# Three moves in the order of work: an early norm, an output's differences, and pinned stretch differences in a two-layer attention kernel

## The chip, the cores and the metric

The kernel runs on one core of a Trainium2 chip. The metric is the device time of one execution in microseconds (us). A core has five instruction queues that matter here: TensorE (PE, matmuls, with its weight loads listed as PEld), VectorE (DVE), ScalarE (ACT), GpSimd (POOL) and SyncE (SP, which issues most DMAs). Each works through its own queue in order and waits on semaphores of the others.

## The reference

The input x is (8, 512, 32, 32) in float32: 8 images of 512 channels and 1024 positions. Two layers follow each other, both with a residual.

```python
# layer 0, 8 heads of 64 channels, group norm over 32 groups
h = group_norm(x); qkv = w_qkv @ h + b_qkv
weight = softmax(q^T k / sqrt(64));  a = weight @ v
x = x + w_proj @ a + b_proj
# layer 1, one head of 512 channels, group norm over 8 groups
h = group_norm(x); q, k, v = w_q h, w_k h, w_v h
x = x + w_p @ (softmax(q^T k / sqrt(512)) v) + b_p
```

## The kernel before

**Products.** Most matrix products (queries, keys, values, projection, layer 1's scores and values) are made with seven block products instead of eight, which needs sums and differences of the blocks first. `image_factors` (it calls `right_sums`, L165) makes the eight differences of an activation of four channel tiles: steps 0 and 1 give t1, 2 and 3 give t2, 4 and 5 overwrite a quarter of the image itself, 6 and 7 give t4. Each step is one VectorE subtraction of 128x512. `inner_factors` (L411) makes differences of these again on GpSimd, for keys and queries. `wino` runs the seven products in a given order, evicts PSUM as it goes, takes a list of `hooks` (one for each product, run after its matmuls are issued) and leaves its last two products, 4 and 3, to be issued after the first product of the next stage (`tail`). Layer 1 uses two products of weights, m (query and key weights) and z (projection and value weights), made once.

**Stages.** `prologue` prepares the weights and makes image 0's v, q, k. Its end, which the change touches, is: the second image's norm (`norm1`, whose statistics are done by then), the transposes of layer 1's value weights (`natural`, L70, into four PSUM banks `tr_wv`), their copies into SBUF (`natv`, L718, two by VectorE and two by ScalarE), the product z (`ps_wz`, 32 matmul passes), the rest of the norm, and the bias products. `group_mean` is a small matmul over the statistics (`gmean`), a copy (L115) and three operations on 128x4 elements (L117, L119, L121). `affine` is another small matmul (`gvar`), one VectorE operation (L126) and four GpSimd operations (L128 to L134).

Then a loop over the images b makes layer 0's attention of image b, with work of other stages between its steps. `attention0` has 8 steps (4 head pairs, two halves of the positions). One step is 16 score matmuls (`sc`), 8 exponentials on ScalarE (`e`, L594), 7 running sums on VectorE (`sum`, L596 and L598), 16 matmuls with the values (`av`), and then the column sums on PE (`sums`), which read the last running sum and whose reciprocal (`rc`, L559) goes out and back by DMA as a row to scale the output on GpSimd (L617). PE issues each matmul in several passes. `extra` is a list of 16 lists of work, one behind the scores and one behind the values of each step. For image 0 it holds the preparation of two weights, the normalization of image 1 (ScalarE, L140), and the eight stretch differences of image 1 (`t_h`, `h`). For a later image it holds layer 1's input of the image before, its stretch differences, and the first four differences of the output a (`t_a`, `a`, L960).

After attention, image 0 makes image 1's values (`values`, stage `psb_v` and others), then the projection (`psa_p`, `psb_p`, `psc_p`) whose block products read the eight differences of a, then image 1's keys and queries. A later image makes its projection and layer 1 of the image before.

**What sets the order.** Matmuls are pinned to the program's order by `keep_in_program_order`. So are some operations of other engines. All others may be moved by the framework's planner, which places an instruction of an engine where it expects its operands. The differences of a are pinned to the program's order before the change, the stretch differences are not.

Of the kernel before, what the change touches and what calls it, by code (L numbers as in the profile page):

```python
# [29 lines left out]
def two_attention_blocks_kernel(  # L30
# [8 lines left out]
    nc = tc.nc  # L39
    B, C, T = x.shape  # L40
    KC = C // P
# [134 lines left out]
    def main_path(ctx):  # L176
# [11 lines left out]
        def pair_tile(name):  # L188
            return big_tile(name, (P, 2, HT))

        def acc_tile(name):
            return ps_acc.tile([P, HT], F32, tag="acc", name=name)
# [509 lines left out]
        def ps_tile(n, name):  # L702
            return acc_tile(name) if n == "acc" else ps_pools["abc".index(n)].tile([P, HT], F32, tag="ps", name=name)
# [7 lines left out]
        def natural(wt, nm, banks):  # L711
            ts_ = [pair_tile(f"nat{nm}_{h}") for h in range(2)]
            t = [ts_[o // 2][:, o % 2, :] for o in range(KC)]
            pt = [ps_tile(banks[o // 2], f"tr_w{nm}_{o}") for o in range(KC)]
            for kc in range(KC):
                for o in range(KC):
                    transpose(pt[o][:, ts(kc, P)], wt[kc][:, ts(o, P)], ident)
            spread(lambda o, copy: tc.keep_in_program_order(copy(t[o], pt[o])), KC)  # L718
            return t
# [34 lines left out]
        def prologue():  # L754
            raw_k = raw("k", 5)
            raw_q = raw("q", 4)
            h0 = [load_x(0, c, "h0") for c in range(KC)]
            first = {n: prepare(n) for n in "vqk"}
            wk = natural(raw_k, "k", ("a", "b"))
            wq = natural(raw_q, "q", ("c", "acc"))  # L760
            norm = GroupNorm(0, "0_0", pinned=True)
            for c in range(KC):
                norm.stats(c, h0[c])
            hf, steps = image_factors(h0, "h0_0")

            def normed():
                norm.affine(acc_tile("gvar_0_0")[:, :KC])
                for c in range(KC):
                    norm.apply(nc.scalar if c % 2 else nc.gpsimd, h0[c], h0[c], c)

            product(
                wq, wk, "m", {6: lambda: norm.group_mean(acc_tile("gmean_0_0")[:, :KC]), 9: normed},
            )
            raw_v = raw("v", 6)
            raw_p = raw("p", 7)
            for f in first["v"][1]:
                f()
            background.extend(steps)
            for n in "qk":
                background.extend(first[n][1])  # L780
            v = by_token(weight_factors(first["v"][0]), hf, "v0_0", middle=(2, 5, 6, 7), back=4)
            finish()
            run_background(len(background))
            keep("v", first["v"][0])
            x1 = [load_x(1, c, "x1") for c in range(KC)] if B > 1 else []
            norm1 = GroupNorm(0, "0_1")
            background.extend(lambda c=c: norm1.stats(c, x1[c]) for c in range(len(x1)))
            q = conv(weight_factors(first["q"][0]), hf, pcols("bq0"), "q0_0")
            keep2("q", first["q"][0])
            keep2("k", first["k"][0])  # L790
            t, steps = prepare("m")
            k = conv(weight_factors(first["k"][0]), hf, pcols("bk0"), "k0_0", hooks=[[], [], [], [], steps])
            finish()
            keep("m", t)
            keep2("m", t)
            norm1.group_mean(acc_tile("gmean_0_1")[:, :KC])
            raw_p0 = raw("p0", 3)
            wv = natural(raw_v, "v", "bc")
            product(wv, raw_p, "z")
            norm1.affine(acc_tile("gvar_0_1")[:, :KC])  # L800
            bias = bias_products([(wk, "bq1"), (raw_p, "bv1"), (raw_p0, "bv0")])
            later = []
            for n in "pz":
                t, steps = prepare(n)
                later.append(steps)
                later.append([lambda n=n, t=t: keep(n, t), load_weight])
            later.append([
                lambda: tc.keep_in_program_order(nc.vector.tensor_copy(ubias, bias[0])),
                lambda: tc.keep_in_program_order(nc.vector.tensor_add(obias[1], bias[1], pcols("bp1"))),
                lambda: tc.keep_in_program_order(nc.vector.tensor_add(obias[0], bias[2], pcols("bp0"))),  # L810
                load_weight,
            ])
            return v, q, k, norm1, later

        psum_pools("first", 2)
        v, q, k, norm0, later = prologue()
# [127 lines left out]
        for b in range(B):  # L944
            extra = [[] for _ in range(2 * 2 * KC)]
            for i, fs in enumerate(later):
                extra[i] += fs
            later = []
            h, loads, applies = [], [], []
            if b > 0:  # L950
                h, loads, applies = begun(load_again, norm1, b - 1, "h1")
            elif B > 1:
                h, loads, applies = begun(load_x, norm0, 1, "h0")
            for f in loads:
                f()
            for i, f in enumerate(applies):
                extra[2 * i + 1].append(f)
            a = channel_tiles(f"a0_{b}")

            af, steps = image_factors(a, f"a_{b}", lambda *t: tc.keep_in_program_order(nc.vector.tensor_sub(*t)))  # L960

            if b > 0:
                hf, t = image_factors(h, f"h1_{b - 1}")
                extra[0] += late
                for i, fs in enumerate((t[:1], t[1:2], (t[2], t[4]), (t[6], t[3]), (t[5], t[7]), steps[:2], steps[2:4])):
                    extra[2 * i + 3] += fs
            elif B > 1:
                hf, t = image_factors(h, "h0_1")
                for i, fs in enumerate((t[:2], (t[2], t[4]), (t[6], t[3]), (t[5], t[7]))):
                    extra[2 * i + 7] += fs  # L970
            psum_pools(f"attention_{b}", 1)
            scaled = attention0(b, q, k, v, a, extra)
            if b > 0:
                for f in steps[4:7]:
                    f()
            psum_pools(f"products_{b}", 2)
            xt = [load_x(b, c, "x") for c in range(KC)]
            if b > 0:

                inner, sums2 = inner_factors(hf, f"h1_{b - 1}", tc.keep_in_program_order)  # L980
                for f in sums2:
                    f()
                norm1, stats = projection(b, af, xt, [scaled, steps[7]])
                gf = layer1_scores(b - 1, hf, inner)
                if b + 1 < B:
                    h, loads, applies = begun(load_x, norm0, b + 1, "h0")
                else:
                    h, loads, applies = begun(load_again, norm1, b, "h1")
                ahead = [loads, *([f] for f in applies)]
                _, *means, affine = norm_hooks(norm1, f"1_{b}")  # L990
                hooks = [[], [], [lambda: background.extend(stats)]], [[], [], *means], affine
                layer1_rest(b - 1, hf, gf, hooks, ahead)
                if b + 1 < B:
                    hf, steps = image_factors(h, f"h0_{b + 1}")
                    background.extend(steps)
                    v, f, norm0 = values(b + 1, hf)
                    q, k, late = keys_and_queries(b + 1, f, norm0, ())
            elif B > 1:
                v, f, norm0 = values(1, hf, [[], steps[:2], steps[2:4], steps[4:6], [steps[6], scaled, steps[7]]])
                norm1, stats = projection(0, af, xt)  # L1000
                hooks = norm_hooks(norm1, "1_0")
                hooks[0].append(lambda: background.extend(stats))
                q, k, late = keys_and_queries(1, f, norm0, hooks)
            else:
                for f in (*steps[:7], scaled, steps[7]):
                    f()
                all_background()
                norm1, stats = projection(0, af, xt)
                finish()
                background.extend(stats)  # L1010
                for f in sum(norm_hooks(norm1, "1_0"), []):
                    f()
                h, loads, applies = begun(load_again, norm1, 0, "h1")
                for f in loads + applies:
                    f()
        hf, steps = image_factors(h, f"h1_{B - 1}")
# [199 lines left out]
```

## Time and profile before

| | |
|---|---|
| median of 3 runs | 2898.86 us (2898.63 to 2899.46) |
| profiled execution | 2901.33 us |
| its span | 2899.5 us |
| PE busy | 2876.1 us |
| DVE, ACT, POOL busy | 2004.1, 922.4, 703.8 us |

The page gives each engine's busy time as a share of the span. The list of waits says who waited for whom, with total, number and longest. A timeline line has the start, the length, the engine, the line, the operation and its tiles, and in brackets the idle time before it and what ended that. A line with xN is a run of N instructions of one kind.

### The profile page before, as it was taken

The page shows a single profiled execution, that of the slowest core. Times are in us where ns is not written, and L with a number is a line of the kernel's source. Part 1 is how long each engine was busy: PE and PEld are TensorE (multiplying, and loading weights), DVE is VectorE, ACT ScalarE, POOL GpSimd, SP SyncE. Part 2 cuts the span into 40 slices and gives each one's busy share as a digit, 9 for nine tenths or more (in the row PEclk, how much of TensorE's full clock was granted, in tenths as well). Part 3 has the DMA queues.
Part 4 walks back from the last instruction along what each step waited for, and adds up shares of the span by engine and source line. Part 5 has one row for each costly group of instructions (what it writes and reads, how often), then busy time and mean ns, then how long its engine had stood idle before and what let it go on. Part 6 is the DMA issues. An engine that isn't in the chain of part 4 may idle for free. (4 is left out here: it accounts for less than half of the span.)

```text
span 2899.5 us, 30282 instructions
## 1 busy us (share of the span) xinstructions
PE 2876.1 (99%) x11132; PEld 1556.2 (54%) x11132; DVE 2004.1 (69%) x2753; ACT 922.4 (32%) x1201; POOL 703.8 (24%) x781
## 2 busy tenths in 40 slices
PE   9999999999999999999999999999999999999999
PEld 5335635566355653556535574356743558345544
DVE  5487787666876678765786657876588665886555
ACT  1252353214532155220552115421163212632110
POOL 2113224032140321403214122232124131140000
PEclk9999999999999999999999999999999999999999
DMA  8622403033031230322213232122311223022201
GB/s 278 223 107 89 176 17 123 32 133 147 19 142 62 107 126 26 131 92 96 107 48 109 92 120 86 48 106 96 139 68 44 105 103 143 27 75 75 95 0 67
DMA packets 91586, 280.91 MB, mean 97 GB/s; under 512 B 10595, under 2 KB 36387, under 8 KB 82470
## 3 DMA queue, kind: packets, MB, share of 16 engines
q1 hardware_dynamic: 89638, 276.61, 26.1%
q10 hardware_dynamic: 1792, 2.29, 0.2%
q8 instruction: 90, 1.47, 0.2%
q14 instruction: 66, 0.54, 0.1%
HBM read 225.93 MB, written 52.93 MB: 96 GB/s over the span
## 5 line engine op out<-in xcount | busy, mean ns | idle before, releaser
L598 DVE TENSOR_TENSOR sum<-sum,e 128x1024 f32<-128x1024 f32 x384 | 519.0, 1351 | 37.9 <-ACT e L594 0.5
L594 ACT ACTIVATE e<-sc 128x1024 f32<-128x1024 f32 x512 | 476.8, 1053 | 74.1 <-PE sc L67 74.1
L67 PE MATMUL sc<-q,k 64*128 64x512 f32 x2048 | 458.3, 596 | 0.0
L67 PE MATMUL av<-e,v 128*64 128x512 f32 x2048 | 453.6, 595 | 0.0
L67 PEld LDWEIGHTS sc<-q,k 64*128 64x128 f32 x2048 | 193.2, 186 | 238.4 <-ACT e L594 105.4
L67 PEld LDWEIGHTS av<-e,v 128*64 128x64 f32 x2048 | 141.4, 137 | 304.3 <-issue 302.3
L561 POOL TENSOR_TENSOR all_recs<-all_recs,rc 128x256 f32<-128x256 f32 x72 | 63.6, 883 | 616.7 <-DVE rc L559 608.9
L617 POOL TENSOR_TENSOR a<-a,r 128x512 f32<-128x512 f32 x56 | 114.1, 2037 | 261.3 <-DMA r<-rows 247.1
L559 DVE RECIPROCAL rc<-sums 128x256 f32<-128x256 f32 x72 | 126.4, 1756 | 57.2 <-PE sums L67 37.7
L612 ACT COPY a<-av 128x512 f32<-128x512 f32 x64 | 37.5, 585 | 305.6 <-PE av L67 305.6
L596 DVE TENSOR_TENSOR sum<-e,e 128x1024 f32<-128x1024 f32 x64 | 78.4, 1224 | 59.0 <-ACT e L594 59.0
L67 PE MATMUL psa_sc<-g,h 128*128 128x512 f32 x256 | 115.2, 595 | 0.0
L648 ACT ACTIVATE e<-e 128x512 f32<-128x512 f32 x96 | 59.7, 629 | 168.5 <-DVE e L647 168.5
L67 PE MATMUL psa_av<-e,z 128*128 128x512 f32 x256 | 113.3, 595 | 0.0
L128 POOL TENSOR_TENSOR rstd<-ve,mhalf 128x4 f32<-128x4 f32 x16 | 36.2, 2261 | 267.8 <-DVE ve L126 267.8
L140 ACT ACTIVATE h<-h,b,s 128x1024 f32<-128x1024 f32 x62 | 78.5, 1268 | 57.7 <-DMA h<-in_x 45.2
L411 POOL TENSOR_TENSOR inner_h<-h,inner_h 128x256 f32<-128x256 f32 x112 | 95.6, 856 | 2.7
L411 POOL TENSOR_TENSOR inner_h<-h 128x256 f32<-128x256 f32 x56 | 57.0, 1019 | 151.3 <-PE psc_av L67 151.3
L444 POOL TENSOR_TENSOR k<-k,k 128x256 f32<-128x256 f32 x28 | 20.1, 728 | 303.6 <-DVE u_k L439 303.6
L67 PEld LDWEIGHTS psa_sc<-g,h 128*128 128x128 f32 x256 | 48.1, 190 | 60.2 <-issue 54.5
L67 PEld LDWEIGHTS psa_av<-e,z 128*128 128x128 f32 x256 | 48.0, 190 | 57.3 <-issue 55.7
L652 POOL COPY sum<-e 128x1024 f32<-128x1024 f32 x8 | 8.8, 1101 | 283.6 <-ACT e L648 283.6
(324 smaller groups left out, 5001.4 us busy)
## 6 DMA issues: line engine op xcount, KB each, us to landing
x<-in_x SPq DMA_DIRECT2D x36, 512.0 KB
h<-in_x SPq DMA_DIRECT2D x32, 512.0 KB
spill<-x SPq DMA_DIRECT2D x32, 512.0 KB
h<-spill SPq DMA_DIRECT2D x32, 512.0 KB
x<-spill SPq DMA_DIRECT2D x32, 512.0 KB
out<-x SPq DMA_DIRECT2D x64, 256.0 KB
w_p<-sums_p SPq DMA_DIRECT2D x8, 1792.0 KB
r<-rows SPq DMA_DIRECT2D x112, 128.0 KB
```

The lines of the kernel that those rows point to most:

```text
L67: tc.keep_in_program_order(nc.tensor.matmul(*args, **kw))
L128: nc.gpsimd.tensor_tensor(rstd, ve, mhalf, ALU.pow)
L140: tc.keep_in_program_order(nc.scalar.activation(dst, src, AF.Identity, bias=b, scale=s))
L411: pin(nc.gpsimd.tensor_tensor(dst, x, y, ALU.subtract))
L559: nc.vector.reciprocal(rc, sums)
L561: nc.gpsimd.tensor_tensor(all_recs, all_recs, rc, ALU.add)
L594: nc.scalar.activation(e, sc, AF.Exp, scale=(C // 8) ** -0.5)
L596: nc.vector.tensor_add(total, es[0], e)
L598: nc.vector.tensor_add(total, total, e)
L612: nc.scalar.copy(dst, av)
L617: nc.gpsimd.tensor_tensor(dst, dst, r, ALU.mult)
L648: nc.scalar.activation(dst, dst, AF.Exp, scale=scale)
```

## The change

Three edits move work and leave the number of instructions as it is.

```diff
@@ prologue
             keep2("m", t)
-            norm1.group_mean(acc_tile("gmean_0_1")[:, :KC])
             raw_p0 = raw("p0", 3)
             wv = natural(raw_v, "v", "bc")
+            norm1.group_mean(acc_tile("gmean_0_1")[:, :KC])
             product(wv, raw_p, "z")
@@ for b in range(B)
-            af, steps = image_factors(a, f"a_{b}", lambda *t: tc.keep_in_program_order(nc.vector.tensor_sub(*t)))
+            here = lambda *t: tc.keep_in_program_order(nc.vector.tensor_sub(*t))
+            af, steps = image_factors(a, f"a_{b}", here)
             if b > 0:
-                hf, t = image_factors(h, f"h1_{b - 1}")
+                hf, t = image_factors(h, f"h1_{b - 1}", here)
...
             elif B > 1:
-                hf, t = image_factors(h, "h0_1")
+                hf, t = image_factors(h, "h0_1", here)
...
-                v, f, norm0 = values(1, hf, [[], steps[:2], steps[2:4], steps[4:6], [steps[6], scaled, steps[7]]])
+                v, f, norm0 = values(1, hf, [[], [], [], [], [*steps[:7], scaled, steps[7]]])
```

- The mean of the second image's norm is taken after the transposes and copies of the value weights instead of before them. On PE the one small matmul moves behind 16 transposes; on VectorE its four operations move behind two copies.
- The differences of image 0's output a, which stood behind products 2, 5, 6 and 7 of image 1's values in groups of two and one, all stand behind product 7.
- The stretch differences of every image are pinned to the program's order. In the built order of VectorE the differences of a step now stand behind the step's last running sum, two at most in a step; before, the planner had put some of them ahead of the last sum (two in image 0's steps at `sum_0_1_1`, `sum_0_2_0` and `sum_0_2_1`, two in one step of each later image, the fifth of eight, and one in two others). Image 0's last two move from an earlier step to the one of `sum_0_3_1`, those of a later image from the fifth step to the sixth. The eight differences of a, after the change, stand in one row behind the first evictions of the values, with one multiplication and two evictions (`v_1_0`, `v_1_1`) among them.

The orders of ScalarE, GpSimd and SP are the same in both kernels, their line numbers aside.

## The prediction

> **What bounds the kernel now.** I read the page first, then TensorE's own list of waits, then the timelines of TensorE, VectorE and GpSimd around each wait.
>
> ```profile
> span 2899.5 us, 30282 instructions
> PE   2876.1 (99%) x11132; PEld 1556.2 (54%) x11132; DVE 2004.1 (69%) x2753; ACT 922.4 (32%) x1201; POOL 703.8 (24%) x781
> ```
>
> TensorE (PE) is busy 99% of the span, so only 23.4 us lie outside its work. No other engine can matter unless it makes PE wait, and a change that leaves the matmuls alone can win only those waits. PE's waits, longest in total first:
>
> ```profile
> PE ps_wz L67 <- issue: 4.4, 1, 4.4
> PE tr_wk L70 <- DMA rawk<-in_w: 3.7, 1, 3.7
> PE psb_v L67 <- DVE u_v L238: 3.6, 1, 3.6
> ```
>
> The second is the first load of the run. The first and third are two single stalls that the change aims at. The first, on PE's, VectorE's and GpSimd's timelines:
>
> ```profile
> 100.54 1.64 PE L70 MATMUL tr_wv<-ident,rawv 128*128 128x128 f32 x13 [0.34 <-DVE k L387]
> 106.56 3.75 PE L67 MATMUL ps_wz<-rawp,natv 128*128 128x512 f32 x4 [4.38 <-issue]
> ```
> ```profile
> 100.59 1.21 DVE L117 TENSOR_TENSOR d<-mv,gmean 128x4 f32<-128x4 f32 x1
> 101.83 2.00 DVE L119 TENSOR_TENSOR d<-d 128x4 f32<-128x4 f32 x1
> 103.86 1.99 DVE L121 TENSOR_TENSOR dv<-d,mv 128x4 f32<-128x4 f32 x1
> 105.78 1.27 DVE L718 COPY natv<-tr_wv 128x512 f32<-128x512 f32 x2
> ```
> ```profile
> 97.53 8.30 POOL L306 TENSOR_TENSOR prepare_m<-prepare_m 128x896 f32<-128x896 f32 x4 [23.89 <-DVE prepare_m L286]
> ```
>
> The transposes of the value weights end at 102.18, and their copies out of PSUM (L718) stand on VectorE behind three 4-column operations of the second image's norm. These take 1.2 to 2.0 us instead of the 0.16 us that the same lines take at 684 us: each ends where one of GpSimd's four 2.07 us operations ends. PE resumes 0.11 us after the first copy. It then runs slowly, which the clock column (after POOL, 0.50 against 1.00) shows:
>
> ```profile
> 106.50:112.30 5.80, 5.74 (x7) 2.50 (x8) 0.55 (x1) 0.00 (x0) 0.00 (x0) 0.50 0.86 257
> 112.30:122.80 10.50, 10.50 (x26) 4.59 (x25) 0.00 (x0) 1.75 (x3) 0.00 (x0) 1.00 0.66 201
> ```
>
> Second stall, VectorE and the last GpSimd operation of that stretch:
>
> ```profile
> 258.00 5.60 DVE L960 TENSOR_TENSOR t_a<-a 128x512 f32<-128x512 f32 x2
> 263.53 0.68 DVE L238 TENSOR_TENSOR u_v<-psb_v,t_v 128x512 f32<-128x512 f32 x1
> ```
> ```profile
> 261.21 1.85 POOL L411 TENSOR_TENSOR inner_h<-t_h,inner_h 128x256 f32<-128x256 f32 x2
> ```
>
> Two differences of image 0's attention output take 5.60 us, against 1.24 us for two of them at 270.47, after GpSimd has ended (263.06). The eviction u_v that PE waits for stands behind them.
>
> A third loss is not in the list of waits, as most of it is too short. PE's sums (the column sums of one attention step) follow each other by 14.65 us, but by 14.86 to 14.88 in ten steps: those whose sums start at 185.22, 200.08, 214.94 in image 0, and one in each later image (414.64, 768.06, and so on). One of them on PE, and VectorE's order there:
>
> ```profile
> 185.22 0.64 PE L67 MATMUL sums<-sum,ones 128*32 128x256 f32 x8 [0.15 <-DVE sum L598]
> ```
> ```profile
> 182.74 1.28 DVE L170 TENSOR_TENSOR t_h<-h 128x512 f32<-128x512 f32 x2
> 183.95 1.22 DVE L598 TENSOR_TENSOR sum<-sum,e 128x1024 f32<-128x1024 f32 x1
> ```
>
> Two stretch differences stand ahead of the step's last sum, which ends at 185.17. PE needed it at about 185.0.
>
> [...] L117 to L121 and L960 wait as above, while L115 (PSUM input) takes 0.15 us and a statistics pass at 247.6 takes 0.63 us with GpSimd busy. [...] The trace agrees on the halving (0.50 after a 4.38 us gap, back to 1.00 near 112.3) and shows that a 3.63 us gap at 260.6 did not trigger it[...].
>
> **The change, part by part.**
>
> *Norm behind the copies.* The mean's matmul goes behind the transposes, and its four VectorE operations behind the two copies. The transposes still wait for VectorE's k (ends 100.48), so they end at 102.18 as before. The first output is complete near 101.83, and VectorE is free: copy one runs from about 101.88 to 102.55 (0.67 us[...]), copy two to 103.15; ScalarE's two end at 103.06 as now. The moved matmul (0.28 us) lies in this wait. PE starts ps_wz at 102.55 + 0.08 = 102.63 instead of 106.56: 3.93 us. The gap left is about 0.4 us, so the clock stays at 1.00 and the 32 passes take 32 x 0.4295 = 13.74 us (0.43 us spacing from 112.5 on), where now 106.56 to 122.77 = 16.21 us: another 2.47 us. Sum 6.40 us. The norm's operations then run from 103.15, and waiting for GpSimd's ends at 103.77 and 105.84 give dv by about 106; its reader, the variance matmul, comes at 102.63 + 13.74 = 116.4. Cover 10 us. GpSimd's four norm operations (1.9 us to 125.6) and SP's queue follow PE: their orders don't change. SP is held by the stores of the prepared weights until 111.16; the first product store would be ready at 110.3, and its load of prepare_p is read 12 us later. If copy one did wait for GpSimd (until 103.77), the part gives 1.2 us less in the first term.
>
> *Differences of image 0 behind the last value product.* The eight subtractions are issued after value product 7 instead of between 5, 6 and 7. VectorE's new order puts statistics passes (single input) before u_v. The second u_v starts at 258.0 + 2 x 0.6 = 259.2 and ends at 259.9, before PE's first half of product 7 ends at 258.74 + 8 x 0.2147 = 260.46. PE goes on there instead of at 264.26: 3.80 us. Next late could be psc_p, whose bank is freed by an eviction behind the whole row. From 259.2 I count, by pitches in this stretch: to w_v 262.4, second w_v 263.1 to 263.7, two evictions to 264.9, then seven subtractions, one multiplication, two evictions and the last subtraction, 11 x 0.6 = 6.6 us, to 271.5, and the eviction needed ends at 272.15. PE asks for it at 260.46 + 1.72 + 3 x 3.45 = 272.5. So 0.35 us of slack; before, PE lost 0.14 us at its start and about 0.1 at its second pass. Sum 3.80 + 0.2 = 4.0 us. GpSimd has ended by 263.1, so the subtractions from 264.9 on take 0.68 us.
>
> *Stretch differences pinned behind the sums.* Same 64 instructions, two per step at most, behind the step's last sum. Ten steps fall from 14.86 to 14.65 us: 10 x 0.21 = 2.1 us. Nothing that PE reads then stands behind them: the reciprocal starts after PE's sums, and sum end 183.95 + two at 0.6 = 185.2 is earlier than that. The pinned subtractions of the output (L960) already stand like that, in steps of 14.65 us. Steps with one difference ahead of the last sum (the one at 723.89) keep 14.65 us, so only the ten with two are counted. Image 0's last two differences move to the step near 229, still before GpSimd first uses them at 239.6; a later image's move from the fifth step to the sixth, ahead of the same GpSimd work. Their ScalarE inputs are applied one step or more ahead.
>
> Together 6.40 + 4.0 + 2.1 = 12.5 us. The profiled execution took 2901.33 us (span 2899.5 and 1.8 around it), which gives 2888.8. The median of the runs shown is 2898.86, 2.47 us lower, which is just the half-clock loss. [...] I take it that the timed runs don't pay it: 2898.86 - 10.0 = 2888.9. If they do, and profiling cost the 2.47 us, it is 2886.4.
>
> **Rivals.**
> - The timed runs pay for the half clock: 2886.4. For it: the three runs agree within 0.8 us, so all or none had it. [...]
> - A wait takes the place of one removed: psc_p behind the row of subtractions (0.35 us of slack only), or copy one behind GpSimd. Losing 1.7 to 4.0 us of the 12.5: 2890.5 to 2892.8.
> - Slower: GpSimd's inner differences are still running when the nine two-input operations come in a row. At (5.60 - 1.24) / 2 = 2.2 us extra each that is 19.8 us, less 0.35 of slack, 19.4 against 12.5 gained: +6.9 us, 2905.8 on the median. It decides when GpSimd ends past 264.9 by most of the row; the trace has it end at 263.06, and nothing delays it.
> - The pins do little, or the order on VectorE is not what hurts, and two parts fail: 2893 to 2897, within 0.2%.
>
> **How the numbers follow.** Forecast 2888.8: 0.63, own range 2887.8 to 2889.9. Half clock paid: 0.14. Replaced wait: 0.15. Two parts fail: 0.05. Slower: 0.03. The range 2885.9 to 2891.3 takes the first two and part of the third, about 0.84. A measurement of this kernel can tell about 0.2% (5.8 us) from no change, so faster means below 2893.1: 0.63 + 0.14 + 0.15 = 0.92, same 0.05, slower 0.03.
>
> **What would show it.** After: ps_wz without a 4.4 us wait, at clock 1.00 throughout, starting near 102.6; dv ending near 106; no psb_v wait on u_v; psc_p starting 4.0 us earlier relative to the attention's last sums; all sums of an attention at 14.65 us; PE's share outside its work down from 23.4 to about 15. Wrong if psc_p or the first score of attention waits on VectorE or a DMA for over 1 us, or if the steps with pinned differences exceed 14.65 us.

## The result, and the profile after

| | before | after |
|---|---|---|
| median in one job (7 runs each) | 2899.46 us (2896.69 to 2901.82) | 2888.66 us (2887.46 to 2889.58) |
| profiled execution | 2901.33 us | 2888.66 us |
| its span | 2899.5 us | 2886.8 us |
| span outside PE's work | 23.4 us | 15.2 us |

The ratio is 0.9962 (95% interval 0.9951 to 0.9974). A later job, with 33 runs of before, gave 2888.75 against 2901.91 us, 0.9953 (0.9939 to 0.9966). The two profiled spans differ by 12.7 us.

The head of the page of after, first the span and then busy time by engine:

```profile
span 2886.8 us, 30280 instructions
...
PE 2871.6 (99%) x11132; PEld 1555.1 (54%) x11132; DVE 2001.5 (69%) x2753; ACT 922.8 (32%) x1201; POOL 704.2 (24%) x781
```

The number of working instructions of each engine is the same; the total is lower by two semaphore instructions. PE's busy time fell by 4.5 us, of which 2.8 us are passes that no longer run at half clock (a granted clock of 0.50, below). Its list of waits (total, number, longest) has lost both stalls:

```profile
PE tr_wk L70 <- DMA rawk<-in_w: 3.8, 1, 3.8
PE psa_v L67 <- issue: 0.8, 1, 0.8
PE psb_v L67 <- DVE w_v L238: 0.5, 1, 0.5
PE tr_wv L70 <- DVE k L387: 0.5, 1, 0.5
PE ps_wm L67 <- DVE natq L718: 0.5, 1, 0.5
PE ps_wz L67 <- ACT natv L718: 0.4, 1, 0.4
```

*First place.* PE's timeline of after:

```profile
100.33 1.64 PE L70 MATMUL tr_wv<-ident,rawv 128*128 128x128 f32 x13 [0.51 <-DVE k L387]
101.81 0.28 PE L67 MATMUL gmean<-mv,gm 128*128 128x4 f32 x2
102.48 13.97 PE L67 MATMUL ps_wz<-rawp,natv 128*128 128x512 f32 x32 [0.39 <-ACT natv L718]
116.29 0.28 PE L67 MATMUL gvar<-dv,gm 128*128 128x4 f32 x2
```

VectorE's timeline beside it:

```profile
101.69 1.29 DVE L718 COPY natv<-tr_wv 128x512 f32<-128x512 f32 x2 [1.41 <-PE tr_wv L70]
102.89 0.15 DVE L115 COPY gmean<-gmean 128x4 f32<-128x4 f32 x1
103.08 0.57 DVE L117 TENSOR_TENSOR d<-mv,gmean 128x4 f32<-128x4 f32 x1
103.68 2.00 DVE L119 TENSOR_TENSOR d<-d 128x4 f32<-128x4 f32 x1
105.71 0.16 DVE L121 TENSOR_TENSOR dv<-d,mv 128x4 f32<-128x4 f32 x1
```

The copies go first and take 0.69 and 0.68 us although GpSimd is in its long row then. The norm behind them still waits for GpSimd (0.57 us in L117, 2.00 us in L119), but nobody waits for it: dv is there at 105.87 and its reader `gvar` comes at 116.29. The clock column (after POOL) says 1.00 where before said 0.50:

```profile
106.50:112.30 5.80, 5.80 (x15) 2.58 (x14) 0.00 (x0) 0.86 (x2) 0.00 (x0) 1.00 0.88 264
```

From the 13 transposes to the first score of attention it is 26.41 us before (100.54 to 126.95) and 19.70 after (100.33 to 120.03): 6.71 us.

*Second place.* VectorE and then PE in after:

```profile
251.60 0.67 DVE L238 TENSOR_TENSOR u_v<-psb_v,t_v 128x512 f32<-128x512 f32 x1
...
257.18 1.28 DVE L960 TENSOR_TENSOR t_a<-a 128x512 f32<-128x512 f32 x2
...
263.79 0.67 DVE L375 TENSOR_TENSOR v<-psc_v,u_v 128x512 f32<-128x512 f32 x1
```
```profile
251.19 3.62 PE L67 MATMUL psb_v<-w_v,h 128*128 128x256 f32 x16
...
264.98 3.60 PE L67 MATMUL psc_p<-t_a,w_p 128*128 128x512 f32 x8
```

The 16 passes of product 7 run in one piece, and psc_p starts without a wait 0.52 us after the eviction that frees its bank (263.79 + 0.67 = 264.46). GpSimd's last difference ends at 255.24, so the row from 257.18 on takes 0.6 us a piece. From image 0's last sums to psc_p it is 32.31 us before and 28.28 after; to the next image's first sums 111.57 and 107.42: 4.15 us.

*Third place.* Two of the sums in after that stood 14.86 us apart before:

```profile
178.08 0.64 PE L67 MATMUL sums<-sum,ones 128*32 128x256 f32 x8
192.74 0.64 PE L67 MATMUL sums<-sum,ones 128*32 128x256 f32 x8
```

The distance is 14.66 us, and 14.65 to 14.66 in every attention. Ten steps of about 0.21 us more are gone, 2.11 us.

6.71 + 4.15 + 2.11 = 13.0 us, against 12.7 us between the spans. One late start in after is of the size of the rest: `psb_k` at 1713.11 us, 0.36 us later against the matmuls ahead of it than in before, behind VectorE's `u_k`.

### The profile page after: what moved, and what is told of

It reads as the page before. It is cut to its first block, busy times and chain, and to the rows that moved or that the text cites. A ratio compares the mean times of both kernels' runs of the same rounds, so it can differ in the third digit from the quotient of the medians.

```text
span 2886.8 us, 30280 instructions
## 1 busy us (share of the span) xinstructions
PE 2871.6 (99%) x11132; PEld 1555.1 (54%) x11132; DVE 2001.5 (69%) x2753; ACT 922.8 (32%) x1201; POOL 704.2 (24%) x781
## 4 chain that ended last, share of the span: by engine, by line
PE 98%; issue 1%; DVE 1%; DMA 0%; POOL 0%; SPq 0%; ACT 0%; DVEq 0%; POOLq 0%
PE sc L67 16%; PE av L67 16%; PE psb_sc L67 6%; PE psb_av L67 6%; PE psa_av L67 4%; PE psa_sc L67 4%; PE psc_av L67 4%; PE psc_sc L67 4%; PE psb_z L67 3%; PE psb_p L67 3%; PE psb_v L67 3%; PE psb_k L67 3%; PE psb_g L67 2%; PE psb_q L67 2%; PE psa_p L67 2%; PE psa_z L67 2%
```

## The experiments

The theory: three separate stalls, each taken away by its own edit, and a half clock that the stalls bring with them. Rivals: only the first edit works and the others ride on it; the timed runs never paid the half clock; the order on VectorE isn't what hurts but GpSimd is; the number of differences ahead of the last sum doesn't matter. Each kernel is given with its median and with that of before in its own job.

### One part alone

**The norm alone**, on before:

```diff
-            norm1.group_mean(acc_tile("gmean_0_1")[:, :KC])
             raw_p0 = raw("p0", 3)
             wv = natural(raw_v, "v", "bc")
+            norm1.group_mean(acc_tile("gmean_0_1")[:, :KC])
```

> Only the first part: the second image's mean behind the value weights' transposes and copies. Theory (the three parts are separate stalls, each worth its own sum): the 4.38 us wait ahead of ps_wz falls to about 0.4 us and PE's clock stays at 1.00 through ps_wz, so the stretch from the transposes to the first attention score is 6.7 us shorter than in the profile of before; the wait of psb_v on u_v (3.6 us) stays, and ten sums stay at 14.86 us. Timed: 4 to 6.7 us under before, depending on how many runs of before pay the half clock. Rival (what is won here is given back at the next stall, as GpSimd's inner differences come earlier against VectorE's work): the wait on u_v grows by several us and the time falls by less than 3 us.

Measured: 2896.27 us against 2901.98, ratio 0.9981 (0.9975 to 0.9988). PE's wait in the second place stays:

```profile
PE psb_v L67 <- DVE u_v L238: 3.7, 1, 3.7
```

Only the first gap went: ps_wz starts after 0.4 us at clock 1.00. But this execution runs at half clock from 258.2 us for 3.41 us, after the second gap. The profiled execution of before did not do that.

**The differences of image 0 alone**, on before:

```diff
-                v, f, norm0 = values(1, hf, [[], steps[:2], steps[2:4], steps[4:6], [steps[6], scaled, steps[7]]])
+                v, f, norm0 = values(1, hf, [[], [], [], [], [*steps[:7], scaled, steps[7]]])
```

> Only the second part: the differences of image 0's output behind the last value product. Theory: the 3.6 us wait of psb_v on u_v goes, psc_p starts 4.0 us earlier against the last sums of image 0's attention, the half clock at ps_wz stays. 4.0 us under before. Rival (the row of differences makes psc_p late instead): psc_p waits for VectorE for over 1 us and the gain is under 3 us.

Measured: 2896.56 us against 2901.98, ratio 0.9984 (0.9977 to 0.9990). Now the first wait stays and the second is gone; psc_p starts 28.28 us after the last sums, as in after.

```profile
PE ps_wz L67 <- issue: 4.4, 1, 4.4
```

**The pins alone**, on before: `here` given to `image_factors(h, ...)` for both kinds of image.

> Only the third part: stretch differences pinned behind the sums. Theory: all sums of an attention follow each other by 14.65 us instead of 14.86 in ten steps, 2.1 us under before, the two single stalls stay. Rival (the pins do nothing of their own, the ten late sums have another cause, such as the exponentials): ten steps stay at 14.86 us and the time stays within 0.5 us.

Measured: 2900.67 us against 2901.98, ratio 0.9995 (0.9987 to 1.0004). By time alone this is inconclusive. By the trace it isn't: all distances between the sums of an attention are 14.65 or 14.66 us, where before has ten of 14.86 to 14.88, and both other waits are there in full.

```profile
PE ps_wz L67 <- issue: 4.4, 1, 4.4
PE psb_v L67 <- DVE u_v L238: 3.7, 1, 3.7
```

The three medians lie 5.7, 5.4 and 1.3 us under before, 12.4 together. Within the noise they add up to the whole, and by the traces each stall goes with its own edit and stays without it: none rides on another.

**After once more**, unchanged, in a job with 33 runs of before:

> The kernel after, unchanged, beside many runs of before on one chip. The three parts measured alone were worth 5.7, 5.4 and 1.3 us, together 12.4. If the parts are independent: 12 to 13 us under the median of before, and a mean clock of 0.999 in its timed runs where before has 0.998. If they overlap: clearly less than 12.

Measured: 2888.75 us (2887.61 to 2889.48) against 2901.91, 13.2 us less.

### Why the copies were late

**GpSimd held back.** The order of before on VectorE, but GpSimd's four operations for m wait for the copies, by one added 128x1 operation that reads them:

```diff
-            keep2("m", t)
             norm1.group_mean(acc_tile("gmean_0_1")[:, :KC])
             raw_p0 = raw("p0", 3)
             wv = natural(raw_v, "v", "bc")
+            held = small.tile([P, 1], F32, tag="held", name="held")
+            tc.keep_in_program_order(nc.gpsimd.tensor_tensor(held, wv[0][:, :1], wv[2][:, :1], ALU.add))
+            keep2("m", t)
```

> Before's order on VectorE (the norm's mean ahead of the copies), with GpSimd's four sums of the m weights held back until the copies are done by one more GpSimd operation on 128x1 elements that reads two of the copies. Theory [...]: the three norm operations take about 0.16 us each, the copies start as soon as the transposes end, the wait ahead of ps_wz is about 0.4 us, the clock stays at 1.00: 4 to 6.7 us under before, the same as moving the norm. Rival (the order itself costs it, or the operations wait for their own inputs): they still take 1.2 to 2 us and the wait ahead of ps_wz stays at 4.4 us.

VectorE, with the norm still ahead of the copies:

```profile
99.92 0.16 DVE L117 TENSOR_TENSOR d<-mv,gmean 128x4 f32<-128x4 f32 x1
100.12 0.16 DVE L119 TENSOR_TENSOR d<-d 128x4 f32<-128x4 f32 x1
100.31 0.17 DVE L121 TENSOR_TENSOR dv<-d,mv 128x4 f32<-128x4 f32 x1
101.22 1.29 DVE L718 COPY natv<-tr_wv 128x512 f32<-128x512 f32 x2 [0.74 <-PE tr_wv L70]
```

0.16, 0.16 and 0.17 us instead of 1.21, 2.00 and 1.99. So GpSimd's row was the cause of these lengths and the order on VectorE only decided who paid.

The kernel took 2898.03 us against 2901.89, ratio 0.9986 (0.9980 to 0.9993): 3.9 us less, and not the 5.7 us of the norm alone. In its profile one step of attention takes 16.24 us instead of 14.88. SP's stores of GpSimd's sums are issued until 114.93 us (until 111.09 with the norm alone). The load of w_p, which waits for another store (`sums_p`), comes at 146.67 instead of 142.59, and behind it in SP's queue the loads of the rows `r` with which GpSimd scales the output. GpSimd then runs three operations back to back beside VectorE's sums of that step. GpSimd, VectorE, and PE at the end of the step:

```profile
169.25 1.26 POOL L617 TENSOR_TENSOR a<-a,r 128x512 f32<-128x512 f32 x1 [10.40 <-DVE sum L598]
170.48 1.71 POOL L561 TENSOR_TENSOR all_recs<-all_recs,rc 128x256 f32<-128x256 f32 x1
172.15 2.26 POOL L617 TENSOR_TENSOR a<-a,r 128x512 f32<-128x512 f32 x1
```
```profile
168.01 8.80 DVE L598 TENSOR_TENSOR sum<-sum,e 128x1024 f32<-128x1024 f32 x5
```
```profile
179.21 0.64 PE L67 MATMUL sums<-sum,ones 128*32 128x256 f32 x8 [1.52 <-DVE sum L598]
```

Three of these five sums take 2.25, 1.57 and 2.11 us. In before, where only one GpSimd operation falls into the same five sums, one takes 2.12 us and the others 1.23, 7.44 us in all. The 1.36 us between 8.80 and 7.44 are what the step is longer by: holding one piece of GpSimd's work back put later GpSimd work in VectorE's way. Moving the norm leaves GpSimd's work, and the stores that wait for it, where they were.

### The half clock in timed runs

**First gap filled.** 32 transposes of the identity, which feed nothing, are added behind `natural` in before:

```diff
             wv = natural(raw_v, "v", "bc")
+            warm = acc_tile("warm")
+            for i in range(32):
+                transpose(warm[:, ts(i % 4, P)], ident, ident)
```

> Before, with 32 more transposes of the identity on PE (3.6 us at 0.114 us each, read by nobody) in the gap between the value weights' transposes and ps_wz. The stall stays, ps_wz starts at about 106.6 as before. Theory (the half clock comes from the idle gap): PE's clock stays at 1.00, ps_wz takes 13.8 us and not 16.6, so the profile shows the first attention score 2.8 us earlier than before; timed, 2.8 us under before if every run of before pays the half clock, 1 to 1.5 us if about half of them do, 0 if the timed runs don't. Rival (the slow passes of ps_wz come from VectorE's late second copy or from data not landed): ps_wz stays at 16.6 us.

PE's timeline: useful work starts as late as in before (6.07 us after the 13 transposes, 6.02 in before) and then runs at full clock.

```profile
102.23 3.66 PE L70 MATMUL warm<-ident 128*128 128x128 f32 x32
106.82 13.97 PE L67 MATMUL ps_wz<-rawp,natv 128*128 128x512 f32 x32 [0.94 <-issue]
120.63 0.28 PE L67 MATMUL gvar<-dv,gm 128*128 128x4 f32 x2
```

From ps_wz to gvar it is 13.81 us. In before it is 16.64 (the same 32 distances). So the half clock cost 2.83 us in the profiled execution of before. The time was 2900.44 us against 2901.98, ratio 0.9996 (0.9988 to 1.0005): inconclusive, and in this execution the second gap brought 3.41 us of half clock of its own.

**Both gaps filled.** So the second gap was filled too, with 30 transposes between the two halves of product 7 (`v0_1`), and 36 in the first:

```diff
+                if (name, p, i) == ("v0_1", 7, 1):
+                    warm = acc_tile("warm2")
+                    for n in range(30):
+                        transpose(warm[:, ts(n % 4, P)], ident, ident)
```

> Before, with 36 extra transposes of the identity in the first gap and 30 in the second, which fill the gaps and feed nothing. Theory A (the timed runs of before pay for half clock after both gaps): the trace has clock 1.00 from 10 us to the end, both starts of useful work as late as in before, and the time is 2.5 to 4.5 us under before, although the kernel does more. Theory B (timed runs don't pay, as the prediction inferred): within 1 us of before.

Measured: 2899.00 us (2898.21 to 2900.52) against 2901.91, ratio 0.9990 (0.9983 to 0.9996). A kernel with 66 matmuls more is 2.9 us faster. The clock is at 1.00 after both gaps, and the useful work starts as late as in before:

```profile
106.09 13.97 PE L67 MATMUL ps_wz<-rawp,natv 128*128 128x512 f32 x32 [0.49 <-issue]
...
260.99 1.99 PE L67 MATMUL psb_v<-w_v,h 128*128 128x256 f32 x8 [0.39 <-DVE u_v L238]
```

So the timed runs of before do pay for half clock, 2.9 us (1.2 to 4.9 by the interval), and 2888.75 is 10.3 us under this kernel: the stalls themselves.

The traces also show how the 2.9 us divide. With the differences alone, the pins alone and both gaps shorter (next), half clock lasts 3.41 us after the first gap, and from ps_wz to gvar it is 15.31 to 15.45 us: 1.5 to 1.6 us of cost. The 2.83 us, after 6.83 us of half clock, stand in the profiled execution of before alone. That execution paid nothing at the second gap, where the norm alone, the pins alone and the first gap filled paid 1.6 us (33.9 us from the last sums to psc_p, 32.31 in before). 1.5 and 1.6 make 3.1. It fits that filling the first gap alone took 1.5 us off, and that the first two parts alone took off 5.7 and 5.4 us: 3.9 of stall and 1.5, 4.0 and 1.6.

**Both gaps shorter.** 12 transposes at the start of the first gap and 6 in the second leave 3.09 and 3.00 us. In the clock record of before, the clock changes 28, 30 and 846 steps of 3.413 us after its first full value; such a step is what the expectation calls a window:

> Before, with 12 extra transposes at the start of the first gap and 6 at the start of the second, which leave gaps of about 3.0 and 2.9 us, under 3.4. If half clock needs one whole window of 3.41 us idle: clock 1.00 throughout, and the same time as with both gaps filled. If it goes by the share of idle time in a window: half clock after at least one gap, and a time nearer to that of before.

Measured: 2903.28 us against 2901.91, ratio 1.0003 (0.9995 to 1.0011): no gain. Stretches of the trace (start and end, length, busy time of PE, PEld, DVE, ACT and POOL, granted clock, DMA share, GB/s):

```profile
107.70:111.20 3.50, 3.48 (x5) 1.69 (x6) 0.52 (x1) 0.00 (x0) 0.00 (x0) 0.56 0.82 244
...
264.10:267.60 3.50, 3.49 (x9) 2.78 (x10) 3.50 (x7) 0.00 (x0) 0.00 (x0) 0.54 0.00 0
```

Half clock follows both gaps (0.56 and 0.54 in these stretches), though PE was idle for only 3.09 and 3.00 us. So a whole step of 3.413 us of idle time was not needed.

### How many differences, and where

**One pair early.** After, with two of the eight differences of a back behind product 2:

```diff
-                v, f, norm0 = values(1, hf, [[], [], [], [], [*steps[:7], scaled, steps[7]]])
+                v, f, norm0 = values(1, hf, [[], steps[:2], [], [], [*steps[2:7], scaled, steps[7]]])
```

> After, with only the first two of the eight differences of image 0's output put back behind value product 2. Theory (what hurt was that the first pair meets GpSimd's row of inner differences ahead of u_v): the wait of psb_v on u_v comes back in full, 3.5 to 4 us, and the time is 4 us over after. Rival (the loss grows with the number of differences issued early): a quarter of it, about 1 us.

Measured: 2894.37 us against 2901.89, ratio 0.9974 (0.9965 to 0.9984), 5.7 us over the first median of after (2888.66). VectorE:

```profile
250.46 5.60 DVE L960 TENSOR_TENSOR t_a<-a 128x512 f32<-128x512 f32 x2
255.99 0.68 DVE L238 TENSOR_TENSOR u_v<-psb_v,t_v 128x512 f32<-128x512 f32 x1
```

The first pair alone brings the whole stall back (3.63 us at psb_v), and half clock from 255.1 us for 6.83 us. No run took GpSimd's row away at this place; that the row is what holds the pair is read from the timelines (last section), and by experiment it is shown only for the prologue.

**Six early.** After, with `[[], steps[:6], [], [], [steps[6], scaled, steps[7]]]`, to price the prediction's slower rival:

> After, with six of the eight differences of image 0's output issued in a row behind value product 2, where GpSimd's inner differences still run for about 4.5 us. Theory A ([...] then the rest run at 0.6 us each): the second u_v comes near 258.6 instead of 251.6, PE's wait there is 5.5 to 6.5 us, and a half clock behind it may add up to 2.9 us: 6 to 9 us over after. Theory B (each of the six pays 2.2 us more, as the prediction priced its slower rival): the wait is 14 us.

Measured: 2897.12 us against 2901.89, ratio 0.9985 (0.9978 to 0.9992). VectorE:

```profile
250.64 5.61 DVE L960 TENSOR_TENSOR t_a<-a 128x512 f32<-128x512 f32 x2
256.18 1.28 DVE L960 TENSOR_TENSOR t_a<-a,t_a 128x512 f32<-128x512 f32 x2
257.38 1.28 DVE L960 TENSOR_TENSOR a<-a,a 128x512 f32<-128x512 f32 x2
258.58 0.68 DVE L238 TENSOR_TENSOR u_v<-psb_v,t_v 128x512 f32<-128x512 f32 x1
```

PE waits 6.0 us: 3.6 as with one pair, and four more differences at 0.6. The pair ends at 256.25, behind the end of GpSimd's row at 255.71, and the four operations behind it paid nothing. That each operation pays 2.2 us is refuted; while GpSimd still ran, several paid in before's prologue: the three of the norm took 1.21, 2.00 and 1.99 us.

**Three ahead of the last sum.** After, with six stretch differences of a later image moved, three at a time, ahead of the last sum of two steps (that sum is pinned as well):

```diff
+                            if s == NS - 1:
+                                for f in ahead.pop((hp, tb), ()):
+                                    f()
+                            tc.keep_in_program_order(nc.vector.tensor_add(total, total, e))
...
+                ahead = {(2, 0): (t[2], t[4], t[6]), (2, 1): (t[3], t[5], t[7])}
```

> After, with six of the stretch differences of each image from the second on put, three each, ahead of the last running sum of the fifth and the sixth step (the sums are pinned). Theory (an operation of 0.6 us ahead of the last sum costs what it exceeds a slack of 1.0 us by; two cost 0.21 us): three cost 0.8 us, 7 images x 2 steps x 0.8 = 11.3 us over after, seen as steps of 15.46 us. Rival (the late sums are not set by what stands ahead of them): the steps stay at 14.65 to 14.86 us, under 3 us.

Measured: 2899.57 us against 2901.89, ratio 0.9993 (0.9984 to 1.0002), 10.9 us over after. PE's waits:

```profile
PE sums L67 <- DVE sum L601: 10.5, 14, 0.8
```

14 steps take 15.46 to 15.48 us, about 0.82 more than 14.65. Two ahead cost 0.21, three cost 0.82, and the third is its own 0.6 us: by estimate VectorE has slack of about 1.0 us in front of the last sum (2 x 0.6 - 0.21). That also tells why one difference ahead costs nothing.

## Why the prediction was right, and where it was off

The time was right, 2888.66 us for 2888.8, and in each of the three places the stall went as described.

*Norm behind the copies*: 6.40 predicted, 6.71 measured. The term of the stall held: ps_wz starts 0.51 us after the transposes' end (101.97), worked out as 0.45, dv came at 105.87 for "by about 106", and copy one did not wait for GpSimd (0.69 us). The mis-sized term is "106.56 to 122.77 = 16.21 us": that is the start of the last pass, 31 distances, set against 32 of 0.4295 us. To gvar, 32 distances, it is 16.64 us; the half clock was worth 2.83 us in that execution and not 2.47. (Another reading is slightly off: the statistics pass at 247.6 took 0.68 us and not 0.63, which changes nothing.)

*Differences of image 0*: 4.0 predicted, 4.03 at psc_p and 4.15 at the next sums. Slack of psc_p 0.35 predicted, 0.52 measured. The rival of the replaced wait had it right that psc_p is next late; it was not late. The sum has no term for half clock behind this stall: the profiled execution had none there, while three of the runs that keep this stall show 1.6 us.

*Pins*: 2.1 predicted, 2.11 measured, on the ten steps named. That single differences ahead of the sum cost nothing held as well.

*The step that failed* is the sentence "I take it that the timed runs don't pay it". It rested on two numbers that agree: the median of the runs shown lies 2.47 us under the profiled execution, and 2.47 us was the half clock. The first was a coincidence of a few runs and the second was mis-sized. 53 of 56 runs of before in the first job of experiments lie at 2900.99 to 2903.34 us, with a mean clock of 0.998 in nearly all, where after has 0.999; and filling both gaps took 2.9 us off. The rival "the timed runs pay" was right that they do. Its number, 2886.4, was off because it put the runs shown, which lie under the usual median of about 2902 us, on top of it. The forecast held because its first sum was made against one execution, whose span, stalls and clock belong together: 2901.33 - 12.5. That the second route, 2898.86 - 10.0 = 2888.9, came out the same was luck: from the usual 2902 us it gives 2892, over 3 us too much. Three runs of before in that job (2896.18 to 2899.79) are faster than the others, two of them faster than any with both gaps filled; in the second job five of 53 lie at 2897.32 to 2899.68. Why isn't settled.

*How often the first gap costs half clock*: it did in all four traces that leave at least 3.09 us of it (6.83 us of half clock in before, 3.41 with the differences alone, with the pins alone and with both gaps shorter). An estimate from the counts of the last section says the same: shared between two steps of 3.413 us, a gap of 4.38 us leaves at least 2.19 us in one of them, and 2.02 us was enough.

*The slower rival* was mispriced, at 2.2 us for each of nine operations. In before the two that took 5.60 us were 4.47 and 1.20 us. With one pair early the two took 5.60 us as well, and with six early the first two took 5.61 and the next four 0.6 each: what was paid was the rest of GpSimd's row (4.4 us over two at 0.6 each), and not a sum for each operation. Half clock included, these two kernels were 5.7 and 8.5 us over after. Both are under the 12.5 gained: at these prices it would not have ended on the slower side.

## What to carry to other kernels

Order the queue of a shared engine by who waits. Here work that nobody needed for 10 us went behind the copy that the busiest engine waited for (6.71 us), and VectorE work of which two operations took 5.60 us beside a GpSimd row went behind the end of the row, where two took 1.28, even though it then piled up in one place (4.15 us). Work a gain out against one profiled execution whose clock and stalls you can see, and add the half clock, which here followed most TensorE gaps of 3.0 to 4.4 us: 10.3 us of stalls were worth 13.2. A queue that has slack for one small operation in each step should be given one and not two: one of 0.6 us ahead of the last sum cost nothing, two cost 0.21 us and three 0.82.

## What the runs showed of the hardware

**When the clock was halved.** In the clock record of every trace, all changes lie on one grid of 3.413 us from the first full clock to the end: in before 28, 30 and 846 steps of it after that clock, in after 842. I counted, for every step of that grid, how long PE was idle in it (from its matmul intervals, whose ends are modelled). At full clock, half clock followed after all eleven steps with at least 2.02 us of idle time (2.02, 2.39, 2.56, 2.68, 2.70, 3.00, 3.06, 3.26 and three at 3.41; of these 2.02 is from one pair early, 3.00 from both gaps shorter, 3.26 from before), and after none with 1.86 or less. At half clock it stayed so after steps with 0.59, 0.77, 1.12 and 1.61 us of idle time and ended after those with up to 0.39. So 59% of a step was enough here. Estimate from these counts for the 3.63 us gap: it escapes only if it is shared so evenly that neither step has more than 1.86 to 2.02 us, which is 0.09 to 0.41 of 3.41 us of positions, 3 to 12%, if all positions are equally likely. The profiled execution of before was such a case (1.83 and 1.81 us), which is why its profile did not show that the second stall costs clock as well.

**A GpSimd row held VectorE past several of its instructions.** In before, the first t_a is issued at 258.00 and ends at 262.48. GpSimd instructions of 0.72 us end at 258.52, 259.20, 259.89, 260.57 and 261.25, and VectorE went ahead only when the next one ended, at 261.93; the last GpSimd instruction then took 1.05 us. It was the same in all nine traces that have the pair there, 4.47 to 4.49 us. The place where VectorE got in is the one pause in that GpSimd row: its last instruction starts 0.08 us after the one before has ended (262.01), where each of the others starts 0.04 us before that end. The pause isn't VectorE's doing, as after has it too (254.50) with no t_a waiting (its first starts at 257.18). But a pause wasn't needed in before's prologue: with instructions of 2.07 us, VectorE got in at the ends of two of them (101.78 and 103.81 us) though the next starts 0.04 us earlier. What makes the difference is open.
